# Two CIN layers: layer 1 from 528 unordered pairs, with x laid out tile by tile

## The chip, the cores and the metric

The kernel runs on one core of one Trainium2 chip. Its metric is the device time of one execution in microseconds; the median of the runs counts. The core's engines work side by side, each on its own queue in order: PE multiplies matrices (PEld is its loading of weights), DVE does elementwise work and reductions, ACT does activations and here empties PSUM, POOL does one instruction, and SP only issues DMAs. Sixteen DMA engines move the data.

## What is computed

The input x has 4096 rows, 32 fields and 16 embedding columns, so 65536 sites (row, embedding). Each layer takes at each site all products of a channel n with a field f and mixes them with weights into 128 channels, followed by a batch norm over all sites. Layer 1 multiplies x with itself, so its product is symmetric in n and f. All is fp32.

```
def _cin_layer(out, x, W, b, gamma, beta):
    h = jnp.einsum('rne,rfe->rnfe', out, x).reshape(r, -1, e)
    h = jnp.einsum('rce,oc->roe', h, W) + b[None, :, None]
    return _batchnorm(h, gamma, beta)          # mean and variance over rows and embedding
h1 = _cin_layer(x, x, W1, ...)                 # 1024 pairs -> 128 channels
out, direct1 = h1[:, :64], h1[:, 64:]
direct2 = _cin_layer(out, x, W2, ...)          # 2048 pairs -> 128 channels
return concatenate([direct1, direct2], 1).sum(-1)
```

## The kernel before

Sites lie along the columns, and one tile is T = 512 of them; there are 128 tiles, `half` 0 or 1 of each of 64 values of `c`. A matmul contracts 128 partitions, a chunk of 128 pairs, into 128 channels by 512 sites (one PSUM buffer). The chunk is an outer product: `a` holds 16 values of n, each repeated on 8 partitions, `b` holds 8 groups of 4 fields, repeated 16 times. The loads make these repeats: `load_b` (L65) reads 32 rows of x 16 times, 1 MB in pieces of 2 KB; each `a` (L110) reads 16 rows 8 times, 256 KB. x lies in HBM as 32 rows of 65536 sites, so a row starts 256 KiB after the one before it. Each queued load waits until its buffer (2 of b, 6 of a) is free.

Layer 1 (L103) runs over c and half. Per tile it loads b and two a, makes three products z of two chunks each on DVE (`outer`, L73; three buffers) and six matmuls on PE (L120). Six chunks suffice for 1024 pairs since the symmetric ones share a matmul under the sum of their weights. ACT then copies the lower 64 channels into the resident tile `hs[c]` (L124) and all 128 into e (L126); DVE takes e's statistics (L127) and sums the upper 64 channels over the embedding (L128).

After the last tile, `batchnorm` turns the statistics into a scale and a shift, and `normalize` (L144) applies them to hs. Layer 2 (L158) runs over the same tiles: it loads b again, spreads 16 rows of hs at a time over 128 partitions with a DMA within SBUF (L167, four a tile), makes two products of two chunks per such a (L73), and 16 matmuls (L172); then one eviction (L176), statistics (L177) and a sum (L178).

The tile framework sets each engine's order and the waits between engines from the code and the pools' buffers, so that work on the next tile stands ahead of the last tile's statistics on DVE.

Of the kernel before, what the change touches and what calls it, by code (L numbers as in the profile page):

```python
# [29 lines left out]
NC = HALF // T  # L30
RT = T // EMB
KEEP = 64
EPS = 1e-5
CHUNKS1 = [(0, 0), (0, 1), (0, 2), (0, 3), (1, 1), (1, 3)]
GROUPS1 = [(0, slice(0, 2)), (0, slice(2, 4)), (1, slice(1, 4, 2))]
# [3 lines left out]
def tile_cin(ctx: ExitStack, tc: tile.TileContext, x, w1, w2, bn, out):  # L39
# [4 lines left out]
    sums = ctx.enter_context(tc.tile_pool(name="sums", bufs=2))  # L44
# [6 lines left out]
    w1_sb = const.tile([P, 8, P], FP, tag="w1", name="w1_sb")  # L51
    nc.scalar.dma_start(w1_sb, w1)
    bn_sb = const.tile([P, 6], FP, tag="bn", name="bn_sb")
    nc.scalar.dma_start(bn_sb, bn)
    w2_sb = const.tile([P, 16, P], FP, tag="w2", name="w2_sb")
    nc.scalar.dma_start(w2_sb, w2)
    b1, g1, beta1, b2, g2, beta2 = (bn_sb[:, k : k + 1] for k in range(6))

    for m, c in ((6, 1), (7, 3)):
        nc.vector.tensor_tensor(w1_sb[:, c, :], w1_sb[:, c, :], w1_sb[:, m, :], ALU.add)  # L60
# [97 lines left out]
    for c in range(NC):  # L158
        if c + 1 < NC:
            normalize(c + 1)  # L160
# [68 lines left out]
```

## Time and profile before

| | |
|---|---|
| median of 3 runs | 2665.64 us |
| lowest and highest run | 2651.52 and 2673.57 us |
| span of the profiled execution | 2674.6 us (the page gives no other time of it) |
| mean granted clock of PE | 0.992 |
| DVE busy | 2009.3 us, 75% of the span |
| ACT busy | 304.2 us, 11% |
| moved by DMA | 475.66 MB, 178 GB/s over the span |
| chain of work that ended last | PE's matmuls of layer 2 66%, issue 33% |

In a row of groups stand line, engine, operation, tiles, shapes and count, then busy time in us and mean of one in ns, then the engine's idle time just before these instructions and who ended most of it. A row of waits names who waited for whom, with the total, the count and the longest. The 40 slices show tenths of busy time, a 9 being 90% or more. "Issue" is time in which PE waited for nothing that the profile shows. A share of DMA above 1 means that packets overlap.

### The profile page before, as it was taken

How to read it: one execution, taken by the hardware profiler on the slowest of the kernel's cores; microseconds unless marked ns; L12 is line 12 of the kernel's file. 1: busy time of each engine (PE TensorE's matmuls, PEld its weight loads, DVE VectorE, ACT ScalarE, POOL GpSimd, SP SyncE). 2: the span in 40 equal slices, each digit the busy share in tenths (PEclk: the TensorE clock that was granted, in tenths of full speed). 3: DMA queues.
4: the chain of work that ended last, by engine and by line, in shares of the span. 5: the costliest groups of instructions: out<-in, count | busy, mean ns of one | idle time of the engine just before them, and what ended most of it. 6: DMA issues, size and time to landing. Idle time of an engine off the chain costs nothing.

```text
span 2674.6 us, 17421 instructions
## 1 busy us (share of the span) xinstructions
PE 2458.1 (92%) x5632; PEld 1064.0 (40%) x5632; DVE 2009.3 (75%) x1946; ACT 304.2 (11%) x452; POOL 2.3 (0%) x5
## 2 busy tenths in 40 slices
PE   6778777878888799999999999999999999999997
PEld 2333333333333344444444444444444444444443
DVE  5677676767777677777777777777777777777776
ACT  1111111211111610000000000000000000000000
POOL 0000000000000000000000000000000000000000
PEclk9999999999999899999999999999999999999998
DMA  9999999999999788888888888888888888888884
GB/s 240 234 232 238 227 224 228 234 230 240 234 235 233 155 155 155 150 150 153 152 156 155 155 152 151 152 149 156 155 155 155 152 151 152 151 156 155 155 154 100
DMA packets 246731, 475.66 MB, mean 178 GB/s; under 512 B 16624, under 2 KB 16624, under 8 KB 246128
## 3 DMA queue, kind: packets, MB, share of 16 engines
q1 hardware_dynamic: 246048, 471.92, 90.1%
q10 hardware_dynamic: 592, 2.62, 0.3%
q8 instruction: 45, 0.74, 0.1%
q14 instruction: 46, 0.38, 0.1%
HBM read 337.12 MB, written 3.15 MB: 127 GB/s over the span
## 4 chain that ended last, share of the span: by engine, by line
PE 66%; issue 33%; DVE 0%; ACT 0%; POOLq 0%; ACTq 0%; DVEq 0%
PE ps L172 66%; DVE mv L79 0%; ACT h L144 0%; POOLq L225 0%; ACTq L149 0%; DVE d L187 0%; DVEq L225 0%; ACT e L176 0%; DVE stats L177 0%; DVE d L178 0%; DVE c L88 0%; DVE ss L91 0%; ACT sd L83 0%; DVE r L85 0%; DVE ss L94 0%
## 5 line engine op out<-in xcount | busy, mean ns | idle before, releaser
L73 DVE TENSOR_TENSOR z<-a,b 128x1024 f32<-128x1024 f32 x1408 | 1689.0, 1222 | 643.3 <-PE ps L172 374.0
L172 PE MATMUL ps<-z,w_sb 128*128 128x512 f32 x4096 | 1760.8, 593 | 16.0 <-ACT h L144 16.0
L172 PEld LDWEIGHTS ps<-z,w_sb 128*128 128x128 f32 x4096 | 779.2, 190 | 997.6 <-issue 980.1
L120 PE MATMUL ps<-z,w_sb 128*128 128x512 f32 x1536 | 697.3, 604 | 184.1 <-DVE z L73 139.6
L120 PEld LDWEIGHTS ps<-z,w_sb 128*128 128x128 f32 x1536 | 284.8, 192 | 595.8 <-issue 318.6
L176 ACT ACTIVATE e<-ps,bn_sb 128x512 f32<-128x512 f32 x128 | 88.0, 688 | 1633.8 <-PE ps L172 1624.7
L124 ACT ACTIVATE h<-ps,bn_sb 64x512 f32<-64x512 f32 x128 | 87.3, 682 | 704.5 <-PE ps L120 704.5
L177 DVE BATCH_NORM_STATS2 stats<-e 128x6 f32<-128x512 f32 x128 | 88.0, 687 | 4.7 <-ACT e L176 4.7
L127 DVE BATCH_NORM_STATS2 stats<-e 128x6 f32<-128x512 f32 x128 | 87.7, 685 | 3.6 <-ACT e L126 3.4
L128 DVE TENSOR_REDUCE d<-e 64x32 f32<-64x512 f32 x128 | 87.3, 682 | 1.8
L126 ACT ACTIVATE e<-ps,bn_sb 128x512 f32<-128x512 f32 x128 | 86.9, 679 | 1.6
L178 DVE TENSOR_REDUCE d<-e 128x32 f32<-128x512 f32 x128 | 85.6, 669 | 0.0
L144 ACT ACTIVATE h<-h,keep 128x512 f32<-128x512 f32 x64 | 45.7, 803 | 3.7 <-issue 1.9
L79 DVE BATCH_NORM_AGGREGATE mv<-stats 128x2 f32<-128x768 f32 x2 | 7.2, 3616 | 0.0
L60 DVE TENSOR_TENSOR w_sb<-w_sb 128x128 f32<-128x128 f32 x2 | 0.5, 288 | 4.7 <-DMA w_sb<-in_w 4.7
L147 POOL TENSOR_SCALAR d<-d,direct 128x2048 f32<-128x2048 f32 x1 | 2.1, 2052 | 890.3 <-DVE direct L141 890.3
L187 DVE TENSOR_SCALAR d<-d,ss 128x2048 f32<-128x2048 f32 x2 | 2.6, 1343 | 0.0
L124 ACT ACT_TABLE_LOAD x1 | 1.3, 1283 | 7.5 <-DMA bn_sb<-in_bn 7.5
L83 ACT ACTIVATE sd<-ve 128x1 f32<-128x1 f32 x2 | 0.4, 202 | 9.1 <-DVE ve L81 9.1
L83 ACT ACT_TABLE_LOAD x1 | 1.3, 1283 | 0.0
L85 DVE RECIPROCAL r<-sd 128x1 f32<-128x1 f32 x2 | 0.3, 164 | 0.5 <-ACT sd L83 0.5
L88 DVE TENSOR_SCALAR c<-r,ve 128x1 f32<-128x1 f32 x2 | 0.5, 272 | 0.1
(12 smaller groups left out, 3.1 us busy)
## 6 DMA issues: line engine op xcount, KB each, us to landing
b<-in_x SPq DMA_DIRECT2D x256, 1024.0 KB, 8.3
a<-h SPq DMA_DIRECT2D x512, 256.0 KB, 5.5
a<-in_x SPq DMA_DIRECT2D x256, 256.0 KB, 9.6
out<-d SPq DMA_DIRECT2D x2, 1024.0 KB, 4.5
w_sb<-in_w ACTq DMA_DIRECT2D x1, 1024.0 KB, 12.4
out<-d ACTq DMA_DIRECT2D x2, 512.0 KB, 8.9
w_sb<-in_w ACTq DMA_DIRECT2D x1, 512.0 KB, 4.0
bn_sb<-in_bn ACTq DMA_DIRECT2D x1, 3.0 KB, 6.3
```

Of the source, the lines that this page charges most:

```text
L73: nc.vector.tensor_tensor(z, a.unsqueeze(1).to_broadcast([P, 2, T]), b[:, js, :], ALU.mult)
L79: nc.vector.bn_aggr(mv, stats.rearrange("p a b -> p (a b)"))
L120: nc.tensor.matmul(ps, w1_sb[:, m, :], z[:, k, :], start=(m == 0), stop=(m == len(CHUNKS1) - 1))
L124: nc.scalar.activation(hs[c][to, :], ps[:KEEP, :], AF.Identity, bias=b1[:KEEP])
L126: nc.scalar.activation(e, ps, AF.Identity, bias=b1)
L127: nc.vector.bn_stats(stats1[:, 2 * c + half, :], e)
L128: nc.vector.tensor_reduce(d1[to, c * RT : (c + 1) * RT], e[KEEP:, :].rearrange("p (r e) -> p r e", e=EMB), AX.X, ALU.add,)
L144: nc.scalar.activation(hs[c], hs[c], AF.Identity, scale=keep[:, 0:1], bias=keep[:, 1:2])
L172: nc.tensor.matmul(ps, w2_sb[:, m, :], z[:, k, :], start=(m == 0), stop=(m == 15))
L176: nc.scalar.activation(e, ps, AF.Identity, bias=b2)
L177: nc.vector.bn_stats(stats2[:, 2 * c + half, :], e)
L178: nc.vector.tensor_reduce(d2[half][:, c * RT : (c + 1) * RT], e.rearrange("p (r e) -> p r e", e=EMB), AX.X, ALU.add,)
```

## The change

Layer 1's 1024 ordered pairs are 528 unordered ones: 512 of them fill four chunks of 128, and the 16 pairs (n, n + 16) are left over. The chunks are pairs (n + 2a, n + 4g + 2 + b) modulo 32 on partition 4n + g, for a, b in 0, 1. One load gives two values of a (each row's 4 KB, four times), another two of b (4 KB out of 48 rows, x wrapped by 16). So one DVE product per tile makes all four chunks, 2048 wide.

The 16 leftover pairs of eight tiles fill 128 partitions, 16 rows a tile, and one DVE product (L148) does them for eight tiles. For four tiles at a time, four matmuls then take 32 partitions each, on rows 0, 32, 64 and 96, into the four tiles' PSUM buffers; the weights of the 16 rows that belong to another tile are zero. Each is the first of its tile's accumulation, and the four full matmuls follow.

ACT evicts three times a tile (all channels, the upper 64 into ed, the lower 64 into hs), and the sum over the embedding is one reduce for both halves. The statistics of a tile are written behind the next tile's matmuls. The mirrored weights are loaded apart and added in one instruction. PSUM has 8 buffers instead of 6.

x is stored three times in HBM, tile by tile: xa (each field beside the field two on), xb (48 wrapped fields), xr (the leftovers' two factors). In layer 2, b is one load of 8 KB pieces, a product is 2048 wide (two z buffers of that width instead of three of half), and its buffers take the memory that layer 1's loads give up.

```diff
-CHUNKS1 = [(0, 0), (0, 1), (0, 2), (0, 3), (1, 1), (1, 3)]
-GROUPS1 = [(0, slice(0, 2)), (0, slice(2, 4)), (1, slice(1, 4, 2))]
+WRAP = 48
+GROUP = 8
...
-    bpool = ctx.enter_context(tc.tile_pool(name="bpool", bufs=2))
-    apool = ctx.enter_context(tc.tile_pool(name="apool", bufs=6))
-    zpool = ctx.enter_context(tc.tile_pool(name="zpool", bufs=3))
-    psum = ctx.enter_context(tc.tile_pool(name="psum", bufs=6, space=bass.MemoryType.PSUM))
+    zpool = ctx.enter_context(tc.tile_pool(name="zpool", bufs=2))
+    psum = ctx.enter_context(tc.tile_pool(name="psum", bufs=8, space=bass.MemoryType.PSUM))
...
+        lpool = one.enter_context(tc.tile_pool(name="lpool", bufs=3))
+        rpool = one.enter_context(tc.tile_pool(name="rpool", bufs=1))
+        def load_rem(g):
+            r = rpool.tile([P, 2 * T], FP, tag="r", name="r")
+            nc.sync.dma_start(r, bass.AP(xr.tensor, xr.offset + g * P * 2 * T, [[2 * T, P], [1, 2 * T]]))
+            return r
+        def load_main(t):
+            a = lpool.tile([P, 2 * T], FP, tag="a", name="a")
+            nc.sync.dma_start(
+                a, bass.AP(xa.tensor, xa.offset + t * FIELDS * 2 * T, [[2 * T, FIELDS], [0, 4], [1, 2 * T]])
+            )
+            b = lpool.tile([P, 2 * T], FP, tag="b", name="b")
+            nc.sync.dma_start(
+                b,
+                bass.AP(xb.tensor, xb.offset + (t * WRAP + 2) * T, [[T, FIELDS], [4 * T, 4], [1, 2 * T]]),
+            )
+            return a, b
...
+        def finish(t):
...
+            nc.scalar.activation(e, ps, AF.Identity, bias=b1)
+            nc.scalar.activation(ed[to, :], ps[KEEP:, :], AF.Identity, bias=b1[KEEP:])
+            nc.scalar.activation(hs[c][to, :], ps[:KEEP, :], AF.Identity, bias=b1[:KEEP])
+            nc.vector.bn_stats(stats1[:, t, :], e)
+            if half == 1:
...
+        for t in range(NT):
+            s = t % GROUP
+            if s == 0:
+                r = load_rem(t // GROUP)
+                zr = rpool.tile([P, T], FP, tag="zr", name="zr")
+                nc.vector.tensor_tensor(zr, r[:, :T], r[:, T:], ALU.mult)
+            a, b = load_main(t)
+            z = zpool.tile([P, 2, 2, T], FP, tag="z", name="z")
+            nc.vector.tensor_tensor(
+                z,
+                a.rearrange("p (a t) -> p a t", a=2).unsqueeze(2).to_broadcast([P, 2, 2, T]),
+                b.rearrange("p (b t) -> p b t", b=2).unsqueeze(1).to_broadcast([P, 2, 2, T]),
+                ALU.mult,
+            )
+            if s % 4 == 0:
+                for k in range(4):
+                    ps = pss[t + k] = psum.tile([P, T], FP, tag="ps", name="ps")
+                    rows = slice(32 * k, 32 * (k + 1))
+                    nc.tensor.matmul(ps, w1_sb[rows, 4 + s // 4, :], zr[rows, :], start=True, stop=False)
+            for m in range(4):
+                nc.tensor.matmul(pss[t], w1_sb[:, m, :], z[:, m // 2, m % 2, :], start=False, stop=(m == 3))
+            if t > 0:
+                finish(t - 1)
...
+        b = bpool.tile([P, 4 * T], FP, tag="b", name="b")
+        nc.sync.dma_start(b, bass.AP(xb.tensor, xb.offset + t * WRAP * T, [[0, 16], [4 * T, 8], [1, 4 * T]]))
...
+            z = zpool.tile([P, 4, T], FP, tag="z", name="z")
+            nc.vector.tensor_tensor(z, a.unsqueeze(1).to_broadcast([P, 4, T]), b, ALU.mult)
```

How the orders move: first PE in the middle of layer 1. The numbers tell buffers apart, and "x4" is four matmuls in a row. Before, three pairs a tile:

```order
L120 MATMUL ps_639<-z_640,w1_sb_79 128x512 x2
L120 MATMUL ps_639<-z_644,w1_sb_79 128x512 x2
L120 MATMUL ps_639<-z_648,w1_sb_79 128x512 x2
L120 MATMUL ps_663<-z_664,w1_sb_79 128x512 x2
L120 MATMUL ps_663<-z_668,w1_sb_79 128x512 x2
L120 MATMUL ps_663<-z_672,w1_sb_79 128x512 x2
```

and after, the same place:

```order
L161 MATMUL ps_973<-zr_893,w1_sb_148 128x512
L161 MATMUL ps_975<-zr_893,w1_sb_148 128x512
L161 MATMUL ps_977<-zr_893,w1_sb_148 128x512
L161 MATMUL ps_979<-zr_893,w1_sb_148 128x512
L163 MATMUL ps_973<-z_971,w1_sb_148 128x512 x4
L163 MATMUL ps_975<-z_995,w1_sb_148 128x512 x4
L163 MATMUL ps_977<-z_1011,w1_sb_148 128x512 x4
L163 MATMUL ps_979<-z_1027,w1_sb_148 128x512 x4
```

Four short-row matmuls (L161) open four PSUM buffers, and 16 full ones fill them. On DVE in layer 1, before (d1 holds the sums):

```order
L73 TENSOR_TENSOR z_448<-a_443,b_441 128x1024
L73 TENSOR_TENSOR z_452<-a_443,b_441 128x1024
L73 TENSOR_TENSOR z_456<-a_445,b_441 128x1024
L127 BN_STATS stats1_152<-e_437 128x6
L128 TENSOR_REDUCE d1_151<-e_437 64x32
```

and after:

```order
L151 TENSOR_TENSOR z_527<-a_523,b_525 128x2048
L132 BN_STATS stats1_138<-e_518 128x6
L151 TENSOR_TENSOR z_551<-a_547,b_549 128x2048
L132 BN_STATS stats1_138<-e_541 128x6
L135 TENSOR_REDUCE d1_137<-ed_517 128x32
L148 TENSOR_TENSOR zr_597<-r_595 128x512
L151 TENSOR_TENSOR z_567<-a_563,b_565 128x2048
```

One product a tile stands where three did, the product of tile t + 2 ahead of the statistics of tile t; the leftovers' product comes once in eight tiles. On DVE in layer 2, after (one tile's b is b_2726, the next one's b_2765):

```order
L208 TENSOR_TENSOR z_2747<-a_2745,b_2726 128x2048
L208 TENSOR_TENSOR z_2755<-a_2753,b_2726 128x2048
L208 TENSOR_TENSOR z_2770<-a_2768,b_2765 128x2048
L208 TENSOR_TENSOR z_2778<-a_2776,b_2765 128x2048
L214 BN_STATS stats2_2566<-e_2761 128x6
L215 TENSOR_REDUCE d2_0_2564<-e_2761 128x32
```

The statistics of a tile stand behind the second product of the next tile, which is as far ahead as two z buffers allow.

More of the change, by code (lines that the diff above doesn't have):

```diff
@@ L100, in tile_cin @@
     d1 = sums.tile([P, ROWS // 2], FP, tag="sum", name="d1")
[L101 to L122 removed]
+    stats1 = const.tile([P, NT, 6], FP, tag="stats", name="stats1")
@@ new lines, in tile_cin @@
+    with ExitStack() as one:
+        wpool = one.enter_context(tc.tile_pool(name="wpool", bufs=1))
+        lpool = one.enter_context(tc.tile_pool(name="lpool", bufs=3))
[15 more added lines that the diff above has]
+            return a, b
+        w1_sb = wpool.tile([P, 6, P], FP, tag="w1", name="w1_sb")
+        nc.scalar.dma_start(w1_sb, w1)
+        w1m_sb = lpool.tile([P, 6, P], FP, tag="a", name="w1m_sb")
+        nc.scalar.dma_start(w1m_sb, w1m)
+        bn_sb = load_bn()
+        w2_sb = const.tile([P, 16, P], FP, tag="w2", name="w2_sb")
+        nc.scalar.dma_start(w2_sb, w2)
+        b1, g1, beta1, b2, g2, beta2 = (bn_sb[:, k : k + 1] for k in range(6))
+        nc.vector.tensor_tensor(w1_sb, w1_sb, w1m_sb, ALU.add)
+        pss = {}
+        eds = {}
+        def finish(t):
+            c, half = divmod(t, 2)
+            ps = pss.pop(t)
@@ L217 @@
     arrays, args = {}, []
[L218 removed]
+    for name, a in (("xa", xa), ("xb", xb), ("xr", xr), ("w1", w1t), ("w1m", w1m), ("w2", w2t), ("bn", bn)):
         a = np.ascontiguousarray(a)
```

148 lines of the change are left out of this document (64 added, 84 removed).

## The prediction

> **What bounds the kernel now.** I read the slices of the span first, then the busy times of the two long stretches, the groups, the waits, and last two stretches of the timeline.
>
> ```profile
> span 2674.6 us, 17421 instructions
> PE   6778777878888799999999999999999999999997
> DMA  9999999999999788888888888888888888888884
> GB/s 240 234 232 238 227 224 228 234 230 240 234 235 233 155 155 155 150 150 153 152 156 155 155 152 151 152 149 156 155 155 155 152 151 152 151 156 155 155 154 100
> ```
>
> The kernel is two stages. In the first thirteen slices (layer 1) the DMA row is full and PE is at seven or eight tenths; from then on (layer 2) PE is full and the DMA is not. A share over the whole span would mix the two. The next rows, each a stretch of the span, make it sharp (columns: stretch, its length, busy time and count of PE, weight loads, DVE, ACT, POOL, then granted clock, DMA share, GB/s).
>
> ```profile
> 20.00:874.00 854.00, 684.80 (x1514) 279.70 (x1513) 602.28 (x630) 165.39 (x252) 0.00 (x0) 0.99 1.06 232
> 906.00:2650.00 1744.00, 1744.00 (x4066) 772.03 (x4065) 1372.27 (x1271) 118.64 (x172) 0.00 (x0) 1.00 0.85 152
> ```
>
> Layer 2's stretch is PE without a gap: 1744 us over 4066 records is 0.429 us a record. One fp32 matmul of the code is two records, so 0.858 us. Layer 1 idles PE for 169 us, and its DMA moves 232 GB/s at a share above one.
>
> ```profile
> L73 DVE TENSOR_TENSOR z<-a,b 128x1024 f32<-128x1024 f32 x1408 | 1689.0, 1222 | 643.3 <-PE ps L172 374.0
> L172 PE MATMUL ps<-z,w_sb 128*128 128x512 f32 x4096 | 1760.8, 593 | 16.0 <-ACT h L144 16.0
> L120 PE MATMUL ps<-z,w_sb 128*128 128x512 f32 x1536 | 697.3, 604 | 184.1 <-DVE z L73 139.6
> L124 ACT ACTIVATE h<-ps,bn_sb 64x512 f32<-64x512 f32 x128 | 87.3, 682 | 704.5 <-PE ps L120 704.5
> L127 DVE BATCH_NORM_STATS2 stats<-e 128x6 f32<-128x512 f32 x128 | 87.7, 685 | 3.6 <-ACT e L126 3.4
> L178 DVE TENSOR_REDUCE d<-e 128x32 f32<-128x512 f32 x128 | 85.6, 669 | 0.0
> DVE z L73 <- DMA b<-in_x: 187.1, 95, 3.0
> PE ps L120 <- DVE z L73: 139.6, 90, 14.9
> ```
>
> The last two rows are waits: layer 1's PE waits for DVE's product, and DVE's product waits for the load of b. One period of it in the timeline (start, length, instruction, idle before):
>
> ```profile
> 299.96 5.39 PE L120 MATMUL ps<-z,w_sb 128*128 128x512 f32 x12 [1.54 <-ACT e L126]
> 305.62 3.50 DVE L73 TENSOR_TENSOR z<-a,b 128x1024 f32<-128x1024 f32 x3 [2.24 <-DMA b<-in_x]
> 307.00 5.39 PE L120 MATMUL ps<-z,w_sb 128*128 128x512 f32 x12 [1.65 <-DVE z L73]
> 14.94 2.08 PE L120 MATMUL ps<-z,w_sb 128*128 128x512 f32 x2 [14.94 <-DVE z L73]
> 874.78 6.67 PE L120 MATMUL ps<-z,w_sb 128*128 128x512 f32 x15
> 897.47 14.99 PE L172 MATMUL ps<-z,w_sb 128*128 128x512 f32 x28 [16.02 <-ACT h L144]
> ```
>
> A tile takes 307.00 - 299.96 = 7.04 us here, of which PE works 5.39. Layer 1 as PE sees it runs from 14.94 to 874.78 + 6.67 = 881.45, which is 866.5 us, 6.77 a tile. That is what the change can shorten; layer 2's 1761 us of PE is the same 2048 matmuls after it.
>
> **Term 1: PE in layer 1.** Six full matmuls a tile become four, and every four tiles share four K=32 matmuls. The four full ones cost 4 x 0.858 = 3.43 us. No row shows a matmul on 32 rows, so I bound it. At the dear end each is priced like a full one: 3.43 us a group of four, 0.86 a tile, 4.29 a tile. At the cheap end all four run beside each other in the time of one: 0.86 a group, 3.65 a tile. I take a value between: each consists of two passes over the same 32 rows, which cannot run beside each other, and if PE starts passes in order, only the second pass of one can overlap the first of the next: five pass times, 5 x 0.429 = 2.15 us. To that I add 0.3 us a group for changing between full array and row tiles: a weight load that no longer hides (192 ns is the mean of a load in the row below) and a drain of about half that. So 2.45 us a group, 0.61 a tile: 4.04 a tile, 128 x 4.04 = 517 us.
>
> ```profile
> L120 PEld LDWEIGHTS ps<-z,w_sb 128*128 128x128 f32 x1536 | 284.8, 192 | 595.8 <-issue 318.6
> ```
>
> The Trainium skill, page "TensorEngine Tiling (Array Packing)", Key Properties, speaks against the change here: changing the tiling mode drains the array. No row before shows a change of mode; at 0.3 us the 32 groups cost 10 us, and the term above holds that already.
>
> **Term 2: does DMA keep up?** A tile now loads 128 x 4 KB for a, as much for b, and an eighth of 512 KB for the leftovers: 1.114 MB, where it was 1.57. At 4.04 us a tile that needs 276 GB/s, and layer 1 has 232. So the question is what a descriptor of 4 KB costs.
>
> ```profile
> DMA packets 11617, 22.44 MB, mean 224 GB/s; under 512 B 673, under 2 KB 673, under 8 KB 11614
> q1 hardware_dynamic: 11614, 22.41, 105.7%
> 9.00:10.00 1.00, 0.00 (x0) 0.00 (x0) 0.00 (x0) 0.00 (x0) 0.00 (x0) 1.00 0.96 319
> 10.00:11.00 1.00, 0.00 (x0) 0.00 (x0) 0.00 (x0) 0.00 (x0) 0.00 (x0) 1.00 1.04 356
> 2669.00:2670.00 1.00, 0.00 (x0) 0.00 (x0) 0.00 (x0) 0.00 (x0) 0.00 (x0) 0.50 0.98 393
> 2671.00:2672.00 1.00, 0.00 (x0) 0.00 (x0) 0.00 (x0) 0.00 (x0) 0.00 (x0) 0.50 1.08 451
> ```
>
> The first two rows are of 300 to 400 us: about 10,940 packets of 2 KB in 100 us on 16 engines, 146 ns each. The last two are the final stores, in 8 KB pieces, at 393 to 451 GB/s: 291 to 333 ns each, 312 in the middle. A straight line through 2 KB and 8 KB gives 201 ns for 4 KB: 326 GB/s, 3.42 us a tile, less than PE's 4.04. The stores go the other way, but the two middle rows, in which w2's 8 KB pieces come in beside x's 2 KB ones, lie at 319 and 356 too. Bounds: 232 GB/s (nothing gained) gives 4.80 us a tile, 393 gives 2.83. I take 326, since both kinds of larger piece in this trace lie nearer to it than to 232. DMA is then hidden under PE; three buffers each of a and b put two tiles of loads ahead.
>
> **Term 3: DVE and ACT in layer 1.** From 512 elements (0.685) to 1024 (1.222) DVE pays 0.537 us, so 2048 cost 1.222 + 2 x 0.537 = 2.30. A tile: product 2.30, bn_stats 0.685, half a reduce 0.33, an eighth of the leftovers' product (a 512-wide one) 0.09: 3.40 us, under 4.04. ACT makes three evictions at 0.682: 2.05. Neither bounds. On DVE the product of tile t+2 stands ahead of the statistics of tile t. It may start once PE has finished tile t (two z buffers), and PE then has 3.43 us or more of tile t+1: product 2.30, then statistics and a reduce. Nothing waits long behind these: in that time ACT has evicted tile t. The new load of r waits for the leftovers' product before it, with the loads of later tiles queued behind it on SP, but that product is several tiles old by then: nothing.
>
> **Term 4: layer 2.** DVE's products there go from 2 x 1.222 to 2.30 a value of i, and the z buffers from three halves to two wholes.
>
> ```profile
> 1503.03 1.23 DVE L73 TENSOR_TENSOR z<-a,b 128x1024 f32<-128x1024 f32 x1 [0.49 <-PE ps L172]
> 1504.80 0.69 ACT L176 ACTIVATE e<-ps,bn_sb 128x512 f32<-128x512 f32 x1 [13.05 <-PE ps L172]
> 1505.89 0.69 DVE L177 BATCH_NORM_STATS2 stats<-e 128x6 f32<-128x512 f32 x1
> 1506.49 0.67 DVE L178 TENSOR_REDUCE d<-e 128x32 f32<-128x512 f32 x1
> ```
>
> A z now feeds PE for 3.43 us. Its successor but one starts when PE is done with it and takes 2.30 of the next 3.43 us; once in four, statistics and reduce follow (start to start 0.60, then 0.6): 3.5 us, so one product starts 0.1 late and still has 1 us in hand. PE keeps its pace: zero. The first product is 1.1 us longer, and PE waits for it: +1. Layer 2's first two loads of b no longer run ahead, since their memory is freed only when layer 1 ends: 2.1 MB at 326 GB/s from about 881 is 6.4 us and some start-up, done before the a loads of the next row are due; at 232 it would be late by about 1.5.
>
> ```profile
> 891.09 16.45 SPq L167 DMA_DIRECT2D a<-h  x9
> ```
>
> ```profile
> 1.00:2.00 1.00, 0.00 (x0) 0.00 (x0) 0.00 (x0) 0.00 (x0) 0.00 (x0) 1.00 0.13 20
> ```
>
> The start: PE's first matmul stood at 14.94 us, after the first loads. Now r, a, b (1.57 MB) and as much of the weights beside them come first, some 3.1 MB; at 326 GB/s that is 9.6 us, with 2 ahead of it in which hardly a byte moves (the row above) and 2.30 for the product: about 14. I take -1 (bounds -5 and +4).
>
> **The sum.** 2674.6 - 866.5 + 517 + 1 - 1 = 2325 for an execution like the profiled one. Its span is 9 us above the median of the three runs (2665.6), so 2316.
>
> **Rivals.**
> *All four row tiles run beside each other.* For it: the four write to four different PSUM buffers from four row strips. Against: weight loads of 0.19 us for each of eight passes, in a row, are 1.5 us by themselves, and no row shows passes overlapping. At 3.65 a tile: 467 us, 2266. It holds only if DMA stays under 3.65. The Trainium skill, "TensorE: Matmul & The Clock Gate", Part 3 (Packing small matmuls), has four row tiles of K=32 at 3.07 times the speed; by that the group would take 1.12 us, the tile 3.71, the run 2274.
>
> *They run one after another.* For it: every matmul in the trace is alone, two passes in turn. 4.29 a tile and 0.08 for the change of mode, 559 us: 2358.
>
> *DMA stays at 232 GB/s.* The rate may come from the reading of the same x rows many times, which stays (4 copies of each a row, 8 overlapping b rows). 4.80 a tile, 615 us: 2414. Against: the middle rows above. The Trainium skill, "DMA: Bandwidth & Descriptors", Latency and other measured facts, says that rows a large power of two apart in HBM are read slowly, 207 GB/s at 512 KiB, and that contiguous tiles are not. Layer 1's rows are 256 KiB apart at 232 GB/s; by the page the new layout would lift the rate by itself.
>
> *Layer 2 loses PE's pace to DVE (slower).* Its whole-width product with two buffers leaves PE idle if it takes longer than (13.73 - 1.3) / 4 = 3.1 us rather than 2.30 (13.73 is PE's 16 x 0.858 a tile, 1.3 the statistics). Each us above that costs 4 us a tile, 512 in all, and each us above 2.94 also lengthens layer 1's tile (2.94 + 1.1 = 4.04), 128 in all: the 349 us saved are gone at 3.6 us. At 4.6 us (twice the estimate) layer 2 is 128 x (18.4 + 1.3 - 13.73) = 764 us longer and layer 1's tile 5.7 us rather than 4.04, 212 more: about 3290. Against: the same kind of broadcast operand is read in L73 at the rate used.
>
> **How the numbers follow.** Chances: the forecast 0.46, all beside each other 0.2, one after another 0.16, DMA 0.13, slower 0.05. The range drops the last two: 2262, just under the cheapest PE, to 2385, past the serial case with the start at its bad end and some waits for DMA. Within 1% is about what a measurement of this kernel cannot tell from no change. All cases but the last end far over 1% faster; of its 0.05, 0.01 is for a DVE product just long enough to cancel the gain: faster 0.95, same 0.01, slower 0.04.
>
> **What would show it.** The full matmuls of layer 1 at 0.43 us a record with DVE's products waiting for PE, not for the load of b; the stretch of layer 1 at about 276 GB/s, 517 us long; some 2.4 us of PE time for each group of K=32 matmuls (0.9 or 3.5 would mean the first or second rival); products at 2.30 us; layer 2's stretch with PE full. If products in layer 1 still wait for loads at a DMA share of one, term 2 is wrong; if PE in layer 2 waits for products, term 4 is.

## The result and the profile after

| | before | after |
|---|---|---|
| median, lowest and highest of 4 runs | 2669.61 us, 2651.52 to 2675.47 | 2290.27 us, 2289.54 to 2290.91 |
| span of the profiled execution | 2674.6 us | 2288.8 us (its own time 2290.6) |
| mean granted clock of PE | 0.992 | 0.993 |

The ratio is 0.8585 (95% interval 0.855 to 0.8621): faster by 14%. The predicted 2316 us was 26 too long; the time lies inside the range of 2262 to 2385.

The first rows of the page of after, the slices of the span:

```profile
span 2288.8 us, 15238 instructions
...
PE   8999999979999999999999999999999999999997
...
DMA  8888888868888888888888888888888888888883
GB/s 316 298 305 295 298 292 301 296 201 158 153 150 151 153 154 155 155 150 151 153 157 155 154 150 151 152 158 154 154 150 151 152 159 154 154 149 151 152 155 92
```

Two stages are still to be seen, and PE is now full in both. Layer 1 takes eight slices and two thirds of the ninth, of 57 us each, where it took thirteen of 67, and its DMA row has gone from nine tenths to eight, although the bytes flow faster. The next rows are two stretches of after, one in each layer (stretch, length, busy time and count of PE, weight loads, DVE, ACT, POOL, then clock, DMA share, GB/s):

```profile
20.00:480.00 460.00, 460.00 (x1224) 193.46 (x1222) 399.30 (x322) 252.29 (x369) 0.00 (x0) 1.00 0.84 297
525.00:2268.00 1743.00, 1743.00 (x4063) 771.66 (x4062) 1308.84 (x762) 115.35 (x167) 0.00 (x0) 1.00 0.83 152
```

PE is busy in the whole of both stretches. The share of DMA in layer 1 is 0.84 at 297 GB/s, where it was 1.06 at 232: an engine that moves more in less of its time has cheaper packets, which is taken up below. The groups of after (line, engine, operation, shapes, count, busy time, mean of one in ns, idle time before and its releaser):

```profile
L211 PE MATMUL ps<-z,w_sb 128*128 128x512 f32 x4096 | 1761.1, 593 | 16.2 <-ACT h L177 16.2
...
L163 PE MATMUL ps<-z,w_sb 128*128 128x512 f32 x1024 | 450.9, 598 | 3.2 <-DVE z L151 3.2
...
L151 DVE TENSOR_TENSOR z<-a,b 128x2048 f32<-128x2048 f32 x128 | 293.4, 2292 | 68.9 <-PE ps L163 65.0
...
L161 PE MATMUL ps<-zr,w_sb 32*128 32x512 f32 x256 | 37.4, 655 | 8.1 <-DVE w_sb L115 8.1
```

Layer 1's matmuls are 450.9 + 37.4 = 488.3 us of PE where they were 697.3, and PE's idle time ahead of them is 3.2 + 8.1 = 11.3 us where it was 184.1. So about 209 us of the gain are matmuls that are not there any more, and about 173 are waits that are not there any more. The order of cause and effect on DVE has turned round: its product now waits for PE, 65.0 us in all, and no longer for the load of b. In the waits of after (who waited for whom: total, count, longest):

```profile
DVE z L151 <- PE ps L163: 65.0, 93, 3.4
...
DVE z L151 <- DMA b<-in_xb: 3.9, 2, 3.0
```

One period of four tiles in the timeline of after, and the three points that bound layer 1 (start, length, instruction, idle before):

```profile
13.41 16.84 PE L163 MATMUL ps<-z,w_sb 128*128 128x512 f32 x32 [3.17 <-DVE z L151]
...
300.21 1.14 PE L161 MATMUL ps<-zr,w_sb 32*128 32x512 f32 x8
301.28 14.00 PE L163 MATMUL ps<-z,w_sb 128*128 128x512 f32 x32
315.21 1.14 PE L161 MATMUL ps<-zr,w_sb 32*128 32x512 f32 x8
...
481.30 14.00 PE L163 MATMUL ps<-z,w_sb 128*128 128x512 f32 x32
511.54 18.65 PE L211 MATMUL ps<-z,w_sb 128*128 128x512 f32 x36 [16.24 <-ACT h L177]
```

From one group of leftovers to the next it is 315.21 - 300.21 = 15.00 us, 3.75 a tile, where the prediction had 4.04. Of the 15.00, the 32 records of full matmuls take 32 x 0.429 = 13.73, so the group of leftovers costs 1.27 us, and not 2.45. Layer 1 runs from 13.41 to 481.30 + 14.00 = 495.30: 481.9 us, against the 517 predicted and the 866.5 before.

How one group runs is seen where the timeline is cut at its first 0.08 us, from 315.20 to 315.28:

```profile
315.21 0.20 PEld L161 LDWEIGHTS ps<-zr,w_sb 32*128 32x128 f32 x4 [0.76 <-issue]
315.21 0.71 PE L161 MATMUL ps<-zr,w_sb 32*128 32x512 f32 x4
```

A pass is one of the two records that a matmul has in the trace. Four of the eight passes have started by then, and four weight loads take 0.20 us together, about as long as one load of a full chunk (0.19). In the trace's records each of these four loads carries a wait, as the load of a matmul's first pass does, and the four loads behind them carry none. So these are the first passes of the four row tiles: they start within 0.02 us, at 315.21 to 315.23, and the four second passes within 0.02 us too, at 315.74 to 315.76. The records also show where more than two pass times go: from the last full pass into the group, to the second passes, out of the group and to the second full pass behind it, the starts lie 0.51 to 0.53 us apart, where full passes in a row lie 0.43 apart.

### The profile page after: what moved, and what is told of

Its sections match the earlier page's. It is cut to its first block, busy times and chain, and to the rows that moved or that the text cites. A ratio compares the mean times of both kernels' runs of the same rounds, so it can differ in the third digit from the quotient of the medians.

```text
span 2288.8 us, 15238 instructions
## 1 busy us (share of the span) xinstructions
PE 2245.0 (98%) x5376; PEld 982.4 (43%) x5376; DVE 1750.0 (76%) x1129; ACT 398.7 (17%) x580; POOL 2.3 (0%) x5
## 4 chain that ended last, share of the span: by engine, by line
PE 77%; issue 22%; DVE 0%; ACT 0%; POOLq 0%; ACTq 0%; DVEq 0%
PE ps L211 77%; ACT h L177 0%; DVE mv L60 0%; POOLq L276 0%; ACTq L182 0%; DVE d L224 0%; DVEq L276 0%; ACT e L213 0%; DVE stats L214 0%; DVE d L215 0%; DVE ss L72 0%; DVE c L69 0%; ACT sd L64 0%; DVE r L66 0%; DVE ss L75 0%
## 5 line engine op out<-in xcount | busy, mean ns | idle before, releaser
L211 PE MATMUL ps<-z,w_sb 128*128 128x512 f32 x4096 | 1761.1, 593 | 16.2 <-ACT h L177 16.2
L208 DVE TENSOR_TENSOR z<-a,b 128x2048 f32<-128x2048 f32 x512 | 1173.0, 2291 | 446.4 <-PE ps L211 439.5
L211 PEld LDWEIGHTS ps<-z,w_sb 128*128 128x128 f32 x4096 | 779.2, 190 | 998.1 <-issue 980.8
L163 PE MATMUL ps<-z,w_sb 128*128 128x512 f32 x1024 | 450.9, 598 | 3.2 <-DVE z L151 3.2
L151 DVE TENSOR_TENSOR z<-a,b 128x2048 f32<-128x2048 f32 x128 | 293.4, 2292 | 68.9 <-PE ps L163 65.0
L163 PEld LDWEIGHTS ps<-z,w_sb 128*128 128x128 f32 x1024 | 193.0, 191 | 259.6 <-issue 251.0
L130 ACT ACTIVATE ed<-ps,bn_sb 64x512 f32<-64x512 f32 x128 | 87.4, 683 | 3.2
L161 PE MATMUL ps<-zr,w_sb 32*128 32x512 f32 x256 | 37.4, 655 | 8.1 <-DVE w_sb L115 8.1
L135 DVE TENSOR_REDUCE d<-ed 128x32 f32<-128x512 f32 x64 | 42.8, 668 | 0.0
L161 PEld LDWEIGHTS ps<-zr,w_sb 32*128 32x128 f32 x256 | 10.2, 186 | 31.7 <-issue 23.5
L148 DVE TENSOR_TENSOR zr<-r 128x512 f32<-128x512 f32 x16 | 10.9, 682 | 6.7 <-DMA r<-in_xr 6.7
L180 POOL TENSOR_SCALAR d<-d,direct 128x2048 f32<-128x2048 f32 x1 | 2.0, 2048 | 503.3 <-DVE direct L174 503.3
```

The source lines that it names most:

```text
L130: nc.scalar.activation(ed[to, :], ps[KEEP:, :], AF.Identity, bias=b1[KEEP:])
L151: nc.vector.tensor_tensor(z, a.rearrange("p (a t) -> p a t", a=2).unsqueeze(2).to_broadcast([P, 2, 2, T]), b.rearrange("p (b t) -> p b t", ...
L161: nc.tensor.matmul(ps, w1_sb[rows, 4 + s // 4, :], zr[rows, :], start=True, stop=False)
L163: nc.tensor.matmul(pss[t], w1_sb[:, m, :], z[:, m // 2, m % 2, :], start=False, stop=(m == 3))
L208: nc.vector.tensor_tensor(z, a.unsqueeze(1).to_broadcast([P, 4, T]), b, ALU.mult)
L211: nc.tensor.matmul(ps, w2_sb[:, m, :], z[:, k, :], start=(m == 0), stop=(m == 15))
```

## The experiments

Four questions were open: what a group of leftovers costs and why, how near DMA stands behind PE, what made DMA quicker, and what the ends of layer 1 still hold. Where no count is given, a kernel ran once. Kernels before ran at 2651 to 2678 us beside them, those like after within 1.4 us, so single runs of the latter kind can be read to a few us.

### What does a group of leftovers cost?

**No leftover matmuls.** The full matmuls alone remain.

```diff
-            if s % 4 == 0:
-                for k in range(4):
-                    ps = pss[t + k] = psum.tile([P, T], FP, tag="ps", name="ps")
-                    rows = slice(32 * k, 32 * (k + 1))
-                    nc.tensor.matmul(ps, w1_sb[rows, 4 + s // 4, :], zr[rows, :], start=True, stop=False)
+            pss[t] = psum.tile([P, T], FP, tag="ps", name="ps")
...
-                nc.tensor.matmul(pss[t], w1_sb[:, m, :], z[:, m // 2, m % 2, :], start=False, stop=(m == 3))
+                nc.tensor.matmul(pss[t], w1_sb[:, m, :], z[:, m // 2, m % 2, :], start=(m == 0), stop=(m == 3))
```

> Leaves out the K=32 matmuls of the 16 leftover pairs; their load and their product on DVE stay. Theory: PE paces layer 1, and a group of four takes 1.27 us there (15.00 us from group to group, less 32 passes of 0.429). Then 32 x 1.27 = 41 us go: 2249 us, 3.43 us a tile, no waits for loads. Rival: DMA is the next bound close behind, at my 326 GB/s or below (3.42 us a tile): then only part of it goes, 2255 to 2275, and DVE's products wait for loads.

Measured: 2255.2 us, a span of 2253.4, which is 35.4 less than after. The first of the 32 groups costs after nothing: it starts at 8.14 us, while PE has to wait for its first product anyway. So 31 groups could go, 39.4 us at 1.27. Where the other 4 are is seen in part in a stretch and in the waits of this kernel:

```profile
20.00:240.00 220.00, 217.33 (x503) 94.62 (x503) 204.24 (x170) 128.60 (x189) 0.00 (x0) 1.00 0.91 326
```

```profile
PE ps L159 <- DVE z L151: 16.0, 8, 13.7
...
DVE zr L148 <- DMA r<-in_xr: 15.3, 13, 5.4
```

PE waits 16.0 us for products, but 13.7 of them are the one wait for the first product, at the start; in layer 1 itself 2.3 us are left, and 0.7 for ACT, where after has none. The leftovers' product waits 15.3 us for its load, where after has 6.7 (5.5 of it at the start), while the products wait 5.7 us for b, hardly more than after's 3.9. So at 3.43 us a tile the loads begin to show, the one of r above all; it has a single buffer, and whether that or DMA's pace is the reason was not tried. The last 1 us is not assigned. The 326 GB/s are 1.114 MB in 3.42 us, which is PE's pace, at a share of 0.91: DMA can do at least that much, and where its limit lies this run doesn't show.

**Leftovers over all 128 rows.** The same number of matmuls, each over the full array, so that each adds up the leftovers of four tiles.

```diff
-                    nc.tensor.matmul(ps, w1_sb[rows, 4 + s // 4, :], zr[rows, :], start=True, stop=False)
+                    nc.tensor.matmul(ps, w1_sb[:, 4 + s // 4, :], zr, start=True, stop=False)
```

> Each leftover matmul runs on all 128 rows (mixing the leftovers of four tiles, which changes what is computed). Theory: the four of a group are cheap only because they run beside each other on four row strips; as full matmuls they take 4 x 0.858 = 3.43 us with no change of mode, 2.16 more than now, 69 us in all: 2359. Rival: the group's cost is mostly something else than passes (the change of mode, waits for PSUM): then the run changes by less than 35 us.

Measured: 2354.77 us, 64.5 more. In its timeline:

```profile
302.87 3.60 PE L161 MATMUL ps<-zr,w_sb 128*128 128x512 f32 x8
306.30 13.90 PE L163 MATMUL ps<-z,w_sb 128*128 128x512 f32 x32
```

A group takes 306.30 - 302.87 = 3.43 us: eight passes of 0.429, one after another, with nothing for a change of mode. So working side by side saves 3.43 - 1.27 = 2.16 us a group, and 32 groups give 69 us, of which 64.5 arrive. Most of the rest is at the start: PE's first 32 full passes take 13.9 us here, behind a long first group, and 16.84 in after.

**One row tile at a time.** The same K=32 matmuls, each ahead of its own tile's full ones, so that none has a neighbour.

```diff
-            if s % 4 == 0:
-                for k in range(4):
-                    ps = pss[t + k] = psum.tile([P, T], FP, tag="ps", name="ps")
-                    rows = slice(32 * k, 32 * (k + 1))
-                    nc.tensor.matmul(ps, w1_sb[rows, 4 + s // 4, :], zr[rows, :], start=True, stop=False)
+            k = s % 4
+            ps = pss[t] = psum.tile([P, T], FP, tag="ps", name="ps")
+            rows = slice(32 * k, 32 * (k + 1))
+            nc.tensor.matmul(ps, w1_sb[rows, 4 + s // 4, :], zr[rows, :], start=True, stop=False)
```

> The same K=32 matmuls, each just ahead of its own tile's four full ones instead of four in a row. Theory: nothing lies beside it, so it costs its two passes, 0.858, and the 0.41 of the change each time: 4.70 us a tile instead of 3.75, 122 us more: 2412. Rival: a matmul on 32 rows is short by itself (a quarter, 0.21): 3.43 + 0.21 + 0.41 = 4.05, 38 more: 2328.

Measured: 2406.08 us, 115.8 more. In its timeline:

```profile
303.17 1.12 PE L160 MATMUL ps<-zr,w_sb 32*128 32x512 f32 x2
304.22 3.70 PE L162 MATMUL ps<-z,w_sb 128*128 128x512 f32 x8
307.85 1.12 PE L160 MATMUL ps<-zr,w_sb 32*128 32x512 f32 x2
```

A tile takes 307.85 - 303.17 = 4.68 us, of which the four full matmuls are 3.43. One row tile alone costs 1.25 us; four together cost 1.27. Three of the four are free, so the four go side by side, in the time that two passes of one take in turn. Since two passes are 0.86 us, 1.25 - 0.86 = 0.39 us and 1.27 - 0.86 = 0.41 us are what going to row tiles and back costs, and it is paid once a group, however many tiles are in it. At 32 groups that is 13 us; with one tile to a group it is paid 128 times.

### How fast can the loads go by themselves?

**One matmul and a narrow product a tile.** PE and DVE were to get out of the way of the loads.

```diff
-            nc.vector.tensor_tensor(
-                z,
...
-            )
+            nc.vector.tensor_tensor(z[:, 0, 0, :], a[:, :T], b[:, :T], ALU.mult)
...
-            for m in range(4):
-                nc.tensor.matmul(pss[t], w1_sb[:, m, :], z[:, m // 2, m % 2, :], start=False, stop=(m == 3))
+            nc.tensor.matmul(pss[t], w1_sb[:, 0, :], z[:, 0, 0, :], start=False, stop=True)
```

> Leaves out three of the four full matmuls of a layer 1 tile and three quarters of its product (DVE 1.8, ACT 2.05, PE about 1.2 us a tile), so that the loads alone set layer 1's pace. Theory by my line through 2 KB and 8 KB pieces: 326 GB/s, 3.42 us a tile, total about 2248. Rival: 297 GB/s, what layer 1 moves now, is all that DMA can: 3.75 a tile, total 2290. Other rival: as fast as the final stores, 393 GB/s, 2.83 a tile, total 2173.

Measured: 2344.58 us, outside of what any of them expected. The run doesn't answer its question. Layer 1 in its stretch and the wait that ruled it:

```profile
20.00:480.00 460.00, 282.90 (x433) 70.37 (x432) 183.15 (x286) 223.53 (x327) 0.00 (x0) 0.55 0.76 265
```

```profile
DVE stats L132 <- ACT e L129: 321.0, 126, 2.9
```

and two tiles of it in the timeline:

```profile
301.15 2.08 PE L157 MATMUL ps<-z,w_sb 128*128 128x512 f32 x2 [2.10 <-DVE z L151]
...
305.32 2.08 PE L157 MATMUL ps<-z,w_sb 128*128 128x512 f32 x2 [2.10 <-DVE z L151]
```

DMA's share is 0.76, so it wasn't the limit. DVE's statistics stand behind ACT's eviction, ACT behind PE, and PE behind the product that DVE issues only after the statistics: one chain through three engines, 305.32 - 301.15 = 4.17 us a tile, with PE at a granted clock of 0.55 and a full matmul at 2.08 us. Layer 1 became longer than with all of its work. The capacity of DMA is read from the first experiment instead: at least 326 GB/s.

### What made the loads quicker?

The prediction put it on larger pieces. The Trainium skill's sentence on rows a power of two apart ("DMA: Bandwidth & Descriptors", Latency and other measured facts) would put it on the layout. These seven kernels take the new loads and the old ones apart.

**Pieces of 2 KB in the changed kernel.** Each load of a and of b in layer 1 becomes two.

```diff
-                a, bass.AP(xa.tensor, xa.offset + t * FIELDS * 2 * T, [[2 * T, FIELDS], [0, 4], [1, 2 * T]])
...
-                bass.AP(xb.tensor, xb.offset + (t * WRAP + 2) * T, [[T, FIELDS], [4 * T, 4], [1, 2 * T]]),
...
+            for k in range(2):
+                to = slice(k * T, (k + 1) * T)
...
+                    bass.AP(xa.tensor, xa.offset + (t * FIELDS * 2 + k) * T, [[2 * T, FIELDS], [0, 4], [1, T]]),
...
+                    bass.AP(xb.tensor, xb.offset + (t * WRAP + 2 + k) * T, [[T, FIELDS], [4 * T, 4], [1, T]]),
...
```

> The changed kernel with a and b of layer 1 loaded in 2 KB pieces (two DMAs of 256 KB each instead of one of 512 KB), from the same tile-by-tile arrays. Theory, piece size: 2 KB pieces take 146 ns as before, 232 GB/s or a little more, 4.6 to 4.8 us a tile, total 2400 to 2425, with products waiting for loads. Rival, layout: the pace of the loads came from where the rows lie; it stays about 300 GB/s or above and the total at 2290 to 2300.

**2 KB pieces from the old layout.** The same two loads each, from rows of x that lie 256 KiB apart.

```diff
...
+            col = (t % 2) * HALF + (t // 2) * T
...
+                    bass.AP(xg.tensor, xg.offset + 2 * k * SITES + col, [[SITES, FIELDS], [0, 4], [1, T]]),
...
+                    bass.AP(xg.tensor, xg.offset + (2 + k) * SITES + col, [[SITES, FIELDS], [4 * SITES, 4], [1, T]]),
...
```

> As the kernel with 2 KB pieces, but layer 1's a and b read from x laid out as before, rows 256 KiB apart; everything else as in the changed kernel. Theory, piece size: no slower than the kernel with 2 KB pieces, 2400 to 2425. Rival, layout: this one alone falls to 232 GB/s, 4.8 us a tile, about 2425, while the kernel with 2 KB pieces stays near 2290. It also tells what the new chunks are worth without the new loads: 240 us or more of the 379.

Measured: 2290.96 and 2291.31 us, against 2290.27. Neither the piece nor the layout is worth more than about a microsecond of this kernel. The same stretch of each (first the 2 KB pieces, then those from the old layout):

```profile
20.00:480.00 460.00, 460.00 (x1224) 194.05 (x1223) 398.81 (x322) 252.31 (x369) 0.00 (x0) 1.00 0.89 297
```

```profile
20.00:480.00 460.00, 460.00 (x1224) 194.05 (x1223) 398.84 (x322) 252.30 (x369) 0.00 (x0) 1.00 0.89 296
```

The smaller pieces raise the share from 0.84 to 0.89 and nothing else; the old layout changes nothing on top of that. Both theories fall for this kernel.

**The new layout in the kernel before**, for a and b. The pieces are still 2 KB (a gap of 16 elements behind each row of b's tile keeps them apart) and b's 16 replicas outermost:

```diff
-            b, bass.AP(x.tensor, x.offset + col, [[0, 16], [SITES, FIELDS], [1, T]])
+            b[:, :, :T],
+            bass.AP(x.tensor, x.offset + col * FIELDS, [[0, 16], [4 * T, 8], [T, 4], [1, T]]),
...
```

> The kernel before with x stored tile by tile, still read in 2 KB pieces (b's tile has a gap after each row so that pieces stay 2 KB). Theory, piece size: no gain, 2660 to 2680. Rival, layout: loads at 300 GB/s and more, layer 1 falls to PE's 5.15 to 5.4 us a tile, total 2460 to 2500.

**The same with b in 8 KB pieces:**

```diff
-            b, bass.AP(x.tensor, x.offset + col, [[0, 16], [SITES, FIELDS], [1, T]])
+            b.rearrange("p j t -> p (j t)"),
+            bass.AP(x.tensor, x.offset + col * FIELDS, [[0, 16], [4 * T, 8], [1, 4 * T]]),
...
```

> The kernel before with x tile by tile and b read in 8 KB pieces, a in 2 KB ones. Theory, piece size: 8 KB pieces at 312 ns and 2 KB ones at 146: 1.05 MB at 420 GB/s and 0.52 at 225 make 4.8 us a tile, under PE's 5.15, so PE paces: 2460 to 2490. Rival, layout: the same as the one with 2 KB pieces, whatever that gives. Third: all 16 replicas of b read the same 8 KB at once and get slower: above 2500.

Measured: 2673.36 and 2653.4 us, both inside the spread of the kernel before. In their stretches of layer 1, in this order:

```profile
20.00:860.00 840.00, 676.44 (x1494) 276.48 (x1492) 593.35 (x621) 162.86 (x249) 0.00 (x0) 0.99 1.05 234
```

```profile
20.00:860.00 840.00, 689.19 (x1529) 281.59 (x1527) 607.28 (x635) 167.60 (x256) 0.00 (x0) 1.00 1.03 238
```

234 and 238 GB/s at a share above one, against 232 before: pieces four times as large in tiles that lie together were read at the old rate. What was left is the order of b's source, by which the text means its steps: which piece each partition gets. Before, the 16 replicas are the outermost step: partitions 0 to 7 read all 32 rows, then 8 to 15 read the same rows again, and so on. In the changed kernel, partition 4n + g starts at row n + 4g. The two also differ in how often a load reads one and the same piece: 16 times before, at most four times in the changed kernel.

**The old order of b in the changed kernel.** As many bytes, in pieces of the same size and from the same layout; only the source's steps change. A load then reads 8 pieces 16 times each, where it read 44 pieces up to four times each, and the products are of other pairs.

```diff
-                bass.AP(xb.tensor, xb.offset + (t * WRAP + 2) * T, [[T, FIELDS], [4 * T, 4], [1, 2 * T]]),
+                bass.AP(xb.tensor, xb.offset + (t * WRAP + 2) * T, [[0, 16], [4 * T, 8], [1, 2 * T]]),
```

> The changed kernel whose layer 1 b is read the way the old b was: 16 replicas outermost, each the same 8 pieces of 4 KB (the wrong pairs, the same bytes). New theory, since piece size and layout both changed nothing: the old b was slow because all 16 DMA engines, one replica each, read the same rows at the same time. From the kernel before: a at 330 GB/s takes 1.6 of the 6.77 us, so b's 1.05 MB took 5.2 us, 202 GB/s; here b's 0.52 MB then takes 2.6 us, the tile 4.4 us, total about 2370, products waiting for b. Rival: who reads what does not matter either, and it is the larger number of bytes or the two buffers of b that held layer 1 back: 2290.

Measured: 2387.64 us, 97.4 more. In its stretch of layer 1 and its waits:

```profile
20.00:440.00 420.00, 371.00 (x930) 145.49 (x929) 301.21 (x243) 190.91 (x279) 0.00 (x0) 0.98 1.01 247
```

```profile
DVE z L151 <- DMA b<-in_xb: 149.2, 113, 4.8
```

The rate is back at 247 GB/s with the share at one, and the product waits for b nearly once a tile, as it did before the change.

**The new order of b in the kernel before**, against the run with 8 KB pieces. Layer 2's b is read in this order too, and the products are of other fields:

```diff
-            bass.AP(x.tensor, x.offset + col * FIELDS, [[0, 16], [4 * T, 8], [1, 4 * T]]),
+            bass.AP(x.tensor, x.offset + col * 48, [[T, FIELDS], [4 * T, 4], [1, 4 * T]]),
...
```

> The kernel before with x tile by tile (48 wrapped rows a tile) and b in 8 KB pieces, as in before_layout_8kb, but b's source goes in the changed kernel's order, partition 4n + g from row n + 4g, instead of 16 replicas of the same 8 pieces (the wrong fields, in both layers). Theory: it is this order of the source that kept layer 1's loads at 232 GB/s, as b_by_replicas shows the other way round; then the loads go to 300 GB/s or more and layer 1 to what PE and DVE allow, 5.2 to 5.5 us a tile, total 2470 to 2510. Rival: the old kernel's loads are held back by something else as well (1.57 MB a tile, the b buffers): 2600 or more.

Measured: 2526.68 us, 126.7 less than with the replicas outermost. In its stretch and its waits:

```profile
20.00:720.00 700.00, 658.40 (x1496) 278.76 (x1495) 596.62 (x623) 163.43 (x250) 0.00 (x0) 1.00 0.87 280
```

```profile
DVE z L74 <- DMA b<-in_x: 82.7, 72, 2.8
...
PE ps L121 <- DVE z L74: 47.5, 46, 12.4
```

The share falls from 1.03 to 0.87 while the rate rises from 238 to 280. The time came out between the two expectations: of PE's waits for products 35.1 us remain behind the first one of 12.4, and products still wait for b. This kernel has two buffers of b where the changed one has three; whether that is the rest was not tried.

In layer 2 the same two kernels show that the order makes the packets dear even where the loads don't set the pace. Replicas outermost, then the new order:

```profile
900.00:2400.00 1500.00, 1500.00 (x3497) 665.50 (x3496) 1180.41 (x1092) 96.98 (x141) 0.00 (x0) 1.00 0.83 153
900.00:2400.00 1500.00, 1500.00 (x3497) 664.12 (x3496) 1181.12 (x1093) 75.68 (x110) 0.00 (x0) 1.00 0.76 154
```

PE is full in both and DMA moves the same, but its share falls from 0.83 to 0.76. Between 1000 and 2400 us, b's 8 KB packets take 569 ns in the mean of the trace's records with replicas outermost, and 399 in the new order. The changed kernel reads layer 2's b with replicas outermost still, at 571 ns; there it is hidden under PE.

**Replicas that start one row apart.** In the kernel before, so that no two replicas read the same row at the same step.

```diff
-            b, bass.AP(x.tensor, x.offset + col, [[0, 16], [SITES, FIELDS], [1, T]])
+            b, bass.AP(x.tensor, x.offset + col, [[SITES, 16], [SITES, FIELDS], [1, T]])
...
```

> The kernel before, whose replica r of b starts at row r instead of row 0, so that the 16 DMA engines read 16 different rows at any time; same bytes, pieces and row pitch (the wrong fields, in both layers). New theory: the loads go from 232 to 300 GB/s or more, layer 1 falls to PE's and DVE's 5.2 to 5.5 us a tile, total 2470 to 2510. Rival, bytes or buffers: nothing changes, 2650 to 2675.

Measured: 2645.24 us, and 244 GB/s in its stretch:

```profile
20.00:440.00 420.00, 350.62 (x779) 143.21 (x778) 309.69 (x325) 85.16 (x130) 0.00 (x0) 1.00 1.06 244
```

That is at most a per cent less, and the share stays above one. If the replicas run side by side, which no row shows, then that all of them ask for one row at one time is not the reason by itself. A load here still reads the same piece up to 16 times.

What a packet costs can be worked out from the DMA queue between 300 and 400 us: the packets of 512 B and more, and the share that they took of 16 engines in 100 us. After, with 2 KB pieces, and with the old order, in this sequence:

```profile
DMA packets 8165, 29.75 MB, mean 298 GB/s; under 512 B 911, under 2 KB 911, under 8 KB 8160
...
q1 hardware_dynamic: 8160, 29.70, 84.3%
```

```profile
DMA packets 15769, 29.64 MB, mean 296 GB/s; under 512 B 1749, under 2 KB 1749, under 8 KB 15763
...
q1 hardware_dynamic: 15763, 29.57, 89.4%
```

```profile
DMA packets 6684, 24.37 MB, mean 244 GB/s; under 512 B 741, under 2 KB 741, under 8 KB 6681
...
q1 hardware_dynamic: 6681, 24.33, 102.7%
```

After has 8160 - 911 = 7249 packets of 4 KB in 16 x 84.3 us: 186 ns each. With 2 KB pieces it is 16 x 89.4 / (15763 - 1749) = 102 ns. The rows of before that the prediction shows give, in the same way, 16 x 105.7 / (11614 - 673) = 155 ns for a 2 KB piece (the prediction's 146 left out that the share is above one). So a 2 KB piece is cheaper by a third in the changed kernel. With the old order there, a 4 KB piece costs 16 x 102.7 / (6681 - 741) = 277 ns instead of 186, half as much again, although only b's half of the pieces is read differently. The pieces of a become dearer with them: by the trace's records half of the 4 KB packets take 159 ns or less in after, while with the old order nine in ten take 233 or more.

### What do the ends of layer 1 hold?

**Ends.** The load of layer 2's weights starts after tile 1 rather than at the start, layer 2's first product comes in a part of 512 and one of 1536, and the last scaling and store come in quarters.

```diff
-        nc.scalar.dma_start(w2_sb, w2)
...
+            if t == 1:
+                nc.scalar.activation(w2_sb[:, 0, 0:1], e[:, 0:1], AF.Identity)
+                nc.scalar.dma_start(w2_sb, w2)
...
-            nc.vector.tensor_tensor(z, a.unsqueeze(1).to_broadcast([P, 4, T]), b, ALU.mult)
+            for lo, hi in ((0, 1), (1, 4)) if t == 0 and i == 0 else ((0, 4),):
+                nc.vector.tensor_tensor(
+                    z[:, lo:hi, :], a.unsqueeze(1).to_broadcast([P, hi - lo, T]), b[:, lo:hi, :], ALU.mult
+                )
...
+        for part in range(2):
+            q = slice(part * (ROWS // 4), (part + 1) * (ROWS // 4))
+            nc.vector.tensor_scalar(d2[half][:, q], d2[half][:, q], ss2[:, 0:1], ss2[:, 2:3], ALU.mult, ALU.add)
...
```

> A try at a faster kernel from what PE still waits for, all of it outside the two loops: w2's 1 MB loads only after tile 1 is done (PE's first full matmul, at 13.4 us, then 2 to 3 us earlier); layer 2's first product in two pieces, 512 and 1536 wide (about 1.5 us less ahead of its first matmul); the final scaling and store in quarters (0.6 us). Theory: 4 to 5 us less than 2290.3, about 2286, 0.2%. Rival: the first loads are not slowed by w2, and only 2 us come: 2288.

Measured: 2285.95 us, median of 5 runs (2285.53 to 2288.18), ratio to before 0.8561 (0.8538 to 0.8584). In its timeline:

```profile
11.77 16.48 PE L165 MATMUL ps<-z,w_sb 128*128 128x512 f32 x32 [1.62 <-DVE z L153]
...
479.29 14.00 PE L165 MATMUL ps<-z,w_sb 128*128 128x512 f32 x32
507.93 22.28 PE L216 MATMUL ps<-z,w_sb 128*128 128x512 f32 x47 [14.64 <-ACT h L179]
```

The first full matmul starts at 11.77 us rather than 13.41, layer 1 ends 2.0 us sooner (481.30 to 479.29), and the wait ahead of layer 2 is 14.64 us rather than 16.24. With 1.2 us less from there to the end, these are the 4.8 us by which the span shrank (2288.8 to 2284.0). Of that 1.2, only 0.1 lies behind the last eviction, where the quarters were to bring 0.6; the other 1.1 is in layer 2's first matmuls (47 passes in 22.28 us, 2.1 more than at 0.429 each, where after has 36 in 18.65, 3.2 more). The slowest of the five runs is quicker than the quickest of after, but the two were run in different series, and the intervals of the two ratios to before overlap: a gain of about 4 us, 0.2%, that points the forecast way but is not settled.

## Why the prediction was right, and where it was off

**What bounds the kernel.** It was read rightly: layer 1 had all there was to win, and layer 2 kept its pace. From layer 2's first matmul to the end it is 2674.6 - 897.47 = 1777.1 us before and 2288.8 - 511.54 = 1777.3 after.

**Term 1, mis-sized.** Four full matmuls at 3.43 us a tile were right. The step that failed is the five pass times of a group, "if PE starts passes in order, only the second pass of one can overlap the first of the next". The trace shows four first passes together and then four second ones, with starts 0.53 us apart: two pass times, 0.86 us, and a part of the change of mode. The price of the change of mode, 0.3, was 0.41. So the group costs 1.27 us and not 2.45, which is 0.32 a tile and not 0.61, and 128 x 0.29 = 37 us too much stood in the sum. With 1.27 in its place the sum is 2288, against a span of 2288.8. The rival in which all four run beside each other was therefore the right mechanism; at 3.65 a tile it was short by the change of mode. The Trainium skill, "TensorE: Matmul & The Clock Gate", Part 3 (Packing small matmuls), has 3.07 times for four row tiles; here it is 3.43 / 1.27 = 2.7 with the change of mode paid once a group, and 3.43 / 0.86 = 4.0 without it. The argument against that rival, that eight weight loads in a row would take 1.5 us, fell too: four row tiles load together.

**Term 2, right for the wrong reason.** DMA does stay hidden, but the forecast was lucky there: the change also altered the order of b's source, and the sum has no term for that. The estimate of 326 GB/s went by the size of the pieces, and 2 KB pieces do as well here (297 GB/s, 2290.96 us). The same figure in the run without the leftover matmuls is no proof of it: there PE's pace asks for just that rate. What had made the pieces dear before, 155 ns against 102, is the order of b's source: given back alone, it costs the changed kernel 97 us, and the new order alone saves a form of the kernel before 127. The rival "DMA stays at 232", with the same x rows read many times as its reason, named the right thing to look at. Four copies of each row of a, and each piece of b read up to four times, were harmless. Every slow kernel here reads a piece of b up to 16 times, and no quick one does, so whether the order or this count makes the price is not shown. Reading the same rows often is not enough by itself: in the new order of the kernel before, a load reads rows 15 to 31 of a tile 16 times as well, in pieces that start at different rows. The Trainium skill's sentence on rows a power of two apart ("DMA: Bandwidth & Descriptors", Latency and other measured facts) doesn't reach down to 256 KiB and pieces of 2 KB: 296 GB/s from such rows and 297 from contiguous tiles, with the time the same within 0.4 us. No run here shows its own case, copies between HBM tensors with a pitch of 512 KiB, for which it gives 207 GB/s. Why replicas outermost are slow stays open. Staggering them by a row hardly helped; how the pieces of such a load fall on the 16 engines and on the memory was not measured.

**Term 3, right.** The product takes 2.29 us (2.30 predicted), ACT's evictions 0.68 each, and neither bounds; products wait for PE.

**Term 4, right in its main point.** Layer 2's PE is full with two wide z buffers. The wait ahead of it grew by 0.2 us rather than 1 (16.02 to 16.24), and the first full matmul came 1.5 us sooner rather than 1.

**The offset of 9 us, wrong.** The prediction carried the distance between before's profiled span and the median of three runs over to the kernel after. That distance was chance of a kernel whose runs spread over 24 us; after's four runs spread over 1.4, and its median lies 1.5 us above its span. Term 1's 37 us too many, this offset's 10.5 too few and the other terms within 1 make up the 26 between 2316 and 2290.

**The slower rival** did not come: a product of 2.29 us is far from the 3.6 at which the gain would have gone.

## What to carry to other kernels

Four pieces of work that each fill a quarter of PE's rows cost what one costs if they stand next to each other in the program, each on its own 32 rows (here also each into its own PSUM buffer; nothing else was tried): the passes go side by side, and the change of mode is paid once a group, so make the groups rare. Where a load repeats its source over partitions and DMA is full at a low rate, try another order of the source before larger pieces or another layout: work out the time of one packet (share x engines x time / packets), since two orders of pieces of one size can differ by half. And take a sum against the profiled execution's own time, without moving the spread of one kernel's runs to another's.

## What the runs showed of the hardware that was not expected

- Four fp32 matmuls on 32 rows each cost 1.27 us together, and a single one 1.25. Going to row tiles and back costs about 0.4 us.
- The order of a load's source moved DMA between 247 and 297 GB/s in one kernel and between 238 and 280 in the other, with as many bytes in pieces of the same size; in the changed kernel rows 256 KiB apart, and pieces of 2 or 4 KB, made no difference to the time.
- Leaving out three quarters of the full matmuls and of the product made layer 1 longer, not shorter: PE, idle between the tiles, was granted a clock of 0.55, and a chain through DVE, PE and ACT took 4.17 us a tile where the whole work takes 3.75.
